# A decoder layer on one core: quantizing the feed-forward weights beside the attention scores, storing through SyncE

## The chip, the cores and the metric

The kernel is one program on one core of a Trainium2 chip. The metric is device time in microseconds (us) of one execution; three executions of the kernel before gave 1202.56, 1204.27 and 1208.85 us, median 1204.27. The engines are named as in the profile: PE is TensorE (PEld its weight loads), DVE is VectorE, ACT is ScalarE, POOL is GpSimd, SP is SyncE. Each engine works through its own instructions in order. Loads and stores between the chip's memory (HBM) and the on-chip memory (SBUF) are issued by SP or by POOL and carried out by the same 16 DMA engines; PE writes only to the eight banks of PSUM.

## The reference

One decoder layer on x of 4 batches x 512 rows x 512 columns, in float32: self-attention, cross-attention, and a feed-forward part whose three weights are first made ternary.

```python
def ternary_quant(w):
    s = jnp.mean(jnp.abs(w))
    q = jnp.clip(jnp.round(w / s), -1.0, 1.0) * s
    return w + jax.lax.stop_gradient(q - w)

# self-attention on layernorm(x), 16 heads; the softmax runs over the 128 columns of q @ k
q = (x @ Wq + bq).reshape(B, T, 128, 16).transpose(0, 3, 2, 1)
k = (x @ Wk + bk).reshape(B, T, 128, 16).transpose(0, 3, 1, 2)
v = (x @ Wv + bv).reshape(B, T, 128, 16).transpose(0, 3, 2, 1)
y = softmax(q @ k / sqrt(128)) @ v            # q @ k is 128 x 128 for each head, y is [B, 16, 128, T]
x = x + y.transpose(0, 2, 1, 3).reshape(B, -1, 2048) @ Wo + bo
# cross-attention of layernorm(x) with the context: 8 heads of 64 rows, softmax over 512 columns
x = x + gamma * vh @ softmax(qh.T @ kh / 8).T
# feed-forward on layernorm(x), hidden size 1365
x = x + (silu(h @ w1q.T) * (h @ w3q.T)) @ w2q.T   # w1q, w3q, w2q = ternary_quant(w1, w3, w2)
```

The ternary weights need two passes over each weight: one that sums absolute values to get the scale, one that compares every element with half the scale.

## The kernel before

**Exact products from halves.** PE multiplies float32r operands. To keep float32 precision each operand is kept as three tiles, called a `Tri`: `h` (a scaled copy, made on ACT), `l` (the rest, on DVE) and `d` (a difference of the two, on DVE; `third_of_weight`, L270, for weights). `products` (L344) runs one 512x512x512 product as two pairs of banks: 16 matmuls of h and l for a pair, a copy of the two banks by ACT (L358), 8 matmuls of d, and `total` (L373) on DVE, which joins copy and bank. It calls a `tick` three times for each pair, six times a product.

**Three phases.** In the *score phase* (L906 to L938) there are 16 steps, `STEPS`, one for each group j of four heads and each batch b. A step computes `keys_of` (one product of the batch's Gram matrix with the key weights of the group), and then the scores of the step before (`scored`, L888), whose softmax weights `turn` (L892) transposes and stores in HBM as `kept_e`. In the *values phase* (L1004 to L1047) there are again 16 steps (b outer, j inner), each with two products (`values_out` with the o weights, `values_of` with the v weights) and `output`, and the cross-attention of the batch before runs beside them in small steps. The *feed-forward phase* (L1107 on) does the rest.

**Work on the side.** A `Side` (L173) is a generator of small steps and a rate: each `tick` of a product takes as many steps as are due. In the score phase the side is `kept_weights` (L286): from the fifth step on (L907), for each of 32 blocks of o and v weights, it loads a raw block (three buffers, two blocks ahead), folds in a mean for v, makes h, l and d (six buffers) and stores all three in HBM (`kept`), all DMAs on POOL (L289, L329), 32 steps over 68 ticks. In the values phase the side `quant` is `quantize` (L661): for w1, w3 and w2 in turn, `quantize_steps` loads 11 or 12 pieces of at most 128x512 through POOL (`staged`, L593, six buffers), sums absolute values on DVE (L628), makes the scales with one small matmul, loads the pieces again, makes them ternary with two DVE instructions (L650, L651) and stores them in HBM (L658). There are 73 steps over 180 ticks. Before each piece, `settle` (L604) multiplies its first column by a one computed from a recent ACT copy (`one_of`, L599), which ties the piece to that copy.

**What sets the order.** SP and POOL issue in program order (L855: `manual_schedule`). PE, ACT and DVE are ordered by a scheduler at build time that follows program order where operands are modelled to be ready; `tc.issue_after(x)` keeps instructions of a block behind instruction x on x's engine. A tile is a buffer of a pool, and whoever writes it anew waits until the last reader is done, a store's landing included. Relevant pools: `made` (six, L324), `raw_k` (`a_kr`, four), the rows `xn` (`a_xn`, eight), the products' weights `a_w` (18, from L976 on) and the staged pieces `a_stage` (six). Weights of the values phase are loaded from `kept` by SP (`weights`, L334), 12 tiles for a product, as far ahead as `a_w` allows.

**Where SP stands.** In the score phase SP loads raw q and k blocks (`raw_all`, L254: a group's whole q after the first scores of that group, its successor's k right behind). At the start of the values phase it loads 12 o tiles, four rows of x, `bo`, 12 v tiles and then `eT` (L1042), for which one of the two `e` buffers must be free: the last two `turn`s come after the first values product (L1017), and their stores go through POOL (L553).

## Time and profile before

| | us |
|---|---|
| median of three runs | 1204.27 |
| lowest, highest | 1202.56, 1208.85 |
| the profiled execution | 1201.91 |
| its span, first to last instruction | 1199.9 |

The granted PE clock is 0.982 of full speed over the span. Busy time of the engines and DMA by phase, read from a table of stretches (74 is the third key product, 293 the end of the score phase, 899 the start of the feed-forward phase):

| stretch, us | PE | DVE | ACT | POOL | clock | DMA share | GB/s |
|---|---|---|---|---|---|---|---|
| 74 to 293 | 215.01 | 155.14 | 93.66 | 84.84 | 0.99 | 0.67 | 223 |
| 293 to 899 | 571.21 | 465.05 | 297.67 | 155.53 | 0.97 | 0.86 | 284 |
| 899 to 1199.9 | 292.40 | 148.78 | 150.25 | 37.18 | 1.00 | 0.19 | 61 |

Over the whole span the page has PE 1148.8 us busy (96%), DVE 817.4, ACT 575.5 and POOL 287.0, and 252.06 MB moved by DMA, 149.21 MB of it in SP's queue and 101.79 MB in POOL's. "Clock" is the share of full PE speed that was granted; "DMA share" is the mean busy share of the 16 DMA engines. PE's busy time includes the modelled tail of pipelined matmuls, so an idle PE is a real gap, but a busy one need not be at full rate; a matmul of 512 columns in these products follows the one before by 0.227 us at full clock and 0.43 at half.

### The profile page before, as it was taken

To read this page: it belongs to the slowest core of one execution; us is meant where nothing else is said; L and a number is where in the kernel's file an instruction comes from. 1 tells how busy PE (TensorE), PEld (TensorE's weight loads), DVE (VectorE), ACT (ScalarE), POOL (GpSimd) and SP (SyncE) were. 2 spreads that over 40 slices of the span, in tenths; PEclk is the share of its full clock that TensorE was granted. 3 is DMA by queue.
4 is the path that set the end of the run, shared out by engine and by line. 5 is a ranking of instruction groups with operands and counts; after the bars stand their busy time and mean duration, and the time that the engine had idled before them with its cause. 6 is when DMAs were issued, how large, how long until landed. Compare 5 with 4: busy or idle time off the path is not lost.

```text
span 1199.9 us, 16588 instructions
## 1 busy us (share of the span) xinstructions
PE 1148.8 (96%) x5406; PEld 888.2 (74%) x5406; DVE 817.4 (68%) x1757; ACT 575.5 (48%) x1156; POOL 287.0 (24%) x515
## 2 busy tenths in 40 slices
PE   8999899999899989999798899998999998999998
PEld 6788788888677667777566676675777776877886
DVE  6657687875577768898759688786886657535242
ACT  4544343443232226557445465563689469733020
POOL 2103363541200233212422221333131311101000
PEclk9999999999899989999899899999999999999999
DMA  9303878787989999977788877898871421221200
GB/s 313 100 9 110 276 262 263 234 278 253 353 315 326 325 297 319 321 224 246 267 270 290 261 239 234 270 342 272 294 232 33 145 80 38 62 79 46 87 1 36
DMA packets 128784, 252.06 MB, mean 210 GB/s; under 512 B 16948, under 2 KB 37732, under 8 KB 128698
## 3 DMA queue, kind: packets, MB, share of 16 engines
q1 hardware_dynamic: 95962, 149.21, 37.5%
q0 software_dynamic: 32736, 101.79, 25.8%
q8 instruction: 43, 0.70, 0.2%
q14 instruction: 43, 0.35, 0.1%
HBM read 196.40 MB, written 54.54 MB: 209 GB/s over the span
## 4 chain that ended last, share of the span: by engine, by line
PE 55%; DMA 15%; issue 12%; DVE 11%; ACT 4%; POOL 4%; SPq 0%; DVEq 0%; POOLq 0%; ACTq 0%
PE h L1124 11%; PE y L1159 7%; PE xo L783 4%; PE xp L127 3%; DMA v_raw<-in_wv_dram 3%; PE po L561 2%; PE sc L520 2%; DMA k_raw<-in_wk_dram 2%; PE xs L739 1%; PE pg L438 1%; PE xs L740 1%; DMA tern_w<-in_w2t_dram 1%; PE pu_3h L351 1%; PE pu_3h L352 1%; DVE xnmax L744 1%
## 5 line engine op out<-in xcount | busy, mean ns | idle before, releaser
L1124 PE MATMUL h<-fxh,t 128*128 128x512 f32 (+1 forms) x352 | 139.9, 398 | 3.2 <-ACT sl L1133 3.2
L1124 PE MATMUL h<-fxl,t 128*128 128x512 f32 (+1 forms) x352 | 137.5, 391 | 0.0
L750 ACT ACTIVATE p<-xs,xnmax 128x512 f32<-128x512 f32 x128 | 87.0, 687 | 68.7 <-PE xp L127 36.4
L744 DVE TENSOR_REDUCE xnmax<-xs 128x1 f32<-128x512 f32 x128 | 84.0, 681 | 10.1 <-PE xs L740 10.1
L1124 PEld LDWEIGHTS h<-fxh,t 128*128 128x128 f32 (+1 forms) x352 | 65.0, 185 | 19.7 <-ACT sl L1133 3.4
L1124 PEld LDWEIGHTS h<-fxl,t 128*128 128x128 f32 (+1 forms) x352 | 65.0, 185 | 14.8 <-DVE fxl L140 0.4
L127 PEld LDWEIGHTS xp<-ident,p 128*128 128x128 f32 x512 | 60.1, 142 | 12.9 <-issue 3.7
L658 POOL DMA_DIRECT2D t_w<-tern_w x43 | 28.6, 666 | 169.9 <-DVE tern_w L651 139.1
L196 ACT ACTIVATE uh<-u 128x512 fp32r<-128x512 f32 x64 | 40.4, 634 | 60.0 <-DVE u L373 59.8
L1159 PE MATMUL y<-t,gh 128*128 128x512 f32 (+1 forms) x176 | 69.0, 392 | 0.0
L1159 PE MATMUL y<-t,gl 128*128 128x512 f32 (+1 forms) x176 | 68.8, 391 | 0.0
L127 PE MATMUL xp<-ident,p 128*128 128x128 f32 x512 | 68.1, 275 | 0.7 <-ACT p L750 0.6
L520 PE MATMUL sc<-y,q_raw 128*128 128x128 f32 x512 | 62.3, 280 | 3.4 <-DVE q_raw L264 3.3
L130 ACT COPY pt<-xp 128x512 f32<-128x512 f32 x96 | 54.7, 590 | 22.5 <-PE xp L127 22.5
L520 PEld LDWEIGHTS sc<-y,q_raw 128*128 128x128 f32 x512 | 61.3, 196 | 5.0 <-DVE q_raw L264 4.0
L1137 DVE SCALAR_TENSOR_TENSOR gf<-h,scales_w,sl 128x512 f32<-128x512 f32 (+1 forms) x44 | 32.9, 747 | 45.2 <-PE h L1124 33.6
L762 ACT ACTIVATE p<-p,xrden 128x512 f32<-128x512 f32 x64 | 47.0, 734 | 27.0 <-DVE xrden L760 26.3
L783 PE MATMUL xo<-pt,vals 128*64 128x512 f32 x256 | 59.5, 599 | 0.2 <-ACT pt L130 0.2
L1133 ACT ACTIVATE sl<-h,scales_w 128x512 f32<-128x512 f32 (+1 forms) x44 | 30.4, 690 | 61.1 <-PE h L1124 61.0
L561 PE MATMUL po<-m,eT 128*128 128x512 f32 x128 | 57.9, 595 | 0.0
L702 POOL DMA_DIRECT2D xd<-x_a x64 | 33.8, 532 | 93.0 <-DVE qs L723 43.1
L739 PE MATMUL xs<-kh,qs 128*128 128x512 f32 x128 | 52.5, 410 | 3.0 <-DVE m L373 1.2
(252 smaller groups left out, 2990.9 us busy)
## 6 DMA issues: line engine op xcount, KB each, us to landing
oh<-kept_oh SPq DMA_DIRECT2D x64, 256.0 KB, 5.1
ol<-kept_ol SPq DMA_DIRECT2D x64, 256.0 KB, 5.2
od<-kept_od SPq DMA_DIRECT2D x64, 256.0 KB, 5.4
vh<-kept_vh SPq DMA_DIRECT2D x64, 256.0 KB, 6.0
vl<-kept_vl SPq DMA_DIRECT2D x64, 256.0 KB, 5.7
vd<-kept_vd SPq DMA_DIRECT2D x64, 256.0 KB, 5.3
xd<-x_a POOLq DMA_DIRECT2D x64, 128.0 KB, 4.3
kd<-in_kv_dram POOLq DMA_DIRECT2D x64, 128.0 KB, 4.2
```

The source lines that it names most:

```text
L127: nc.tensor.transpose(pt[:, ts(k, P)], src[:, ts(k, P)], ident)
L130: nc.scalar.copy(dst, pv)
L196: nc.scalar.mul(tri.h, src, H_OF)
L520: nc.tensor.matmul(sc[:, ts(g, DH)], lhsT=w[k][:, ts(g, DH)], rhs=ys[k][:, ts(g, DH)], start=(k == 0), stop=(k == KC - 1),)
L561: nc.tensor.matmul(po, lhsT=eT[:, ts(g, DH)], rhs=ms[g], start=True, stop=True)
L739: nc.tensor.matmul(sc, lhsT=q[:, ts(m, P)], rhs=kh, start=True, stop=False)
L744: nc.vector.reduce_max(nmax[:, i : i + 1], scs[i], axis=AX.X)
L750: nc.scalar.activation(p, scs[i], AF.Exp, bias=nmax[:, i : i + 1], scale=xscale, accum_out=den[:, i : i + 1],)
L762: nc.scalar.mul(ps[1], ps[1], rden[:, 1:2])
L783: nc.tensor.matmul(po[half, :], lhsT=vals[c][:, l, half], rhs=pt[j][:, l, :], start=(l == 0), stop=(l == NC - 1),)
L1124: nc.tensor.matmul(ph[:r, :], lhsT=t[:, block(i, k)], rhs=fxT[j][:, k, :], start=(k == 0 and j == 0), stop=(k == KC - 1 and j == 1),)
L1159: nc.tensor.matmul(py, lhsT=g[i][j][:r, ts(c, P)], rhs=t2[:r, i, :], start=(i == 0 and j == 0), stop=(i == NHC - 1 and j == 1),)
```

## The change

The quantizing moves from the values phase to the score phase, and the shares of the engines in the side work are set anew:

- `quantize` runs from the third score step on (n == 2), 108 steps over 82 ticks, with three staged pieces instead of six. Its absolute sums are ACT activations (`Abs` with an accumulator) behind the last bank copy, two pieces ahead; the ternary pass stays on DVE, behind the last `total`, one piece ahead, and its stores come one step later. `settle` is no longer called for the pieces. Loads and stores of the pieces stay on POOL.
- `kept_weights` starts at n == 2 instead of 4, with 64 steps over 80 ticks (making and storing a block are steps of their own). `d` is made on POOL; four `made` buffers instead of six; its loads and stores go through SP.
- The stores of `kept_e` go through SP. `turn`s are placed at ticks inside the products; the last two come at ticks 4 and 6 of the first values product.
- A group's last scores follow its last key product at once, the next group's q is loaded there, and q is folded at tick 2. Raw k blocks have three buffers, and the fourth block is loaded later. For the first group it lies in a ninth `xn` buffer.
- The values phase has no quantizing; its weight pool has 24 buffers instead of 18. The rows of x for its first product are loaded and split during the last three score steps.
- Twelve small memsets go from DVE to POOL.

```diff
-    def third_of_weight(tri):
-        nc.vector.tensor_tensor(tri.d, tri.l.bitcast(F32), tri.h.bitcast(F32), ALU.subtract)
+    def third_of_weight(tri, engine=None):
+        (engine or nc.vector).tensor_tensor(
+            tri.d, tri.l.bitcast(F32), tri.h.bitcast(F32), ALU.subtract
+        )
...
     def kept_weights(pool):
-
-        def load(dst, src):
-            nc.gpsimd.dma_start(dst, src)
...
-                *(pool.tile([P, GW], F32R, tag="made", bufs=6, name=f"{n}{p}_{j}_{k}") for p in "hld")
+                *(pool.tile([P, GW], F32R, tag="made", bufs=4, name=f"{n}{p}_{j}_{k}") for p in "hld")
             )
             halves_of_weight(tri.h, tri.l, t, gate)
-            third_of_weight(tri)
+            third_of_weight(tri, nc.gpsimd)
+            yield
             for p, part in zip("hld", (tri.h, tri.l, tri.d)):
-                nc.gpsimd.dma_start(kept[n, j, p][ts(k, P), :], part.bitcast(F32))
+                load(kept[n, j, p][ts(k, P), :], part.bitcast(F32))
             yield
-    KEPT_STEPS = 2 * HG * KC
+    KEPT_STEPS = 2 * 2 * HG * KC
...
-                nc.vector.memset(xs[g][:, D - 1 : D], 1.0)
+                (nc.vector if by_chunk else nc.gpsimd).memset(xs[g][:, D - 1 : D], 1.0)
...
-        nc.gpsimd.dma_start(kept_e[b, j], e)
+        load(kept_e[b, j], e)
...
-    def ahead(pieces, name):
-
-        coming = None
-        for i, (src, t) in enumerate([*pieces, (None, None)]):
-            here, coming = coming, src is not None and (staged(src, f"{name}_{i}"), t, i)
-            if here:
-                settle(here[0])
-                yield here
+    def ahead(pieces, name, by):
+
+        coming = []
+        for i, piece in enumerate([*pieces, *[None] * by]):
+            if piece is not None:
+                coming.append((staged(piece[0], f"{name}_{i}"), piece[1], i))
+            if i >= by:
+                yield coming.pop(0)
...
-        for piece, t, i in ahead(pieces, f"abs_{name}"):
-            nc.vector.tensor_reduce(
-                sums[: piece.shape[0], i : i + 1],
-                piece,
-                AX.X,
-                ALU.add,
-                apply_absolute_value=True,
-            )
+        for piece, t, i in ahead(pieces, f"abs_{name}", 2):
+            r, n = piece.shape
+            spare = stp.tile([P, 512], BF16, tag="above", bufs=1, name=f"spare_{name}_{i}")
+            with tc.issue_after(mark["copied"]):
+                nc.scalar.activation(
+                    spare[:r, :n], piece, AF.Abs, accum_out=sums[:r, i : i + 1]
+                )
             yield
...
-        for piece, t, i in ahead(pieces, f"tern_{name}"):
+        for piece, t, i in ahead(pieces, f"tern_{name}", 1):
             r, n = piece.shape
             above = stp.tile([P, 512], BF16, tag="above", bufs=1, name=f"above_{name}_{i}")
-            nc.vector.tensor_scalar(above[:r, :n], piece, s[:r, 0:1], None, ALU.is_gt)
-            nc.vector.scalar_tensor_tensor(
-                piece, piece, s[:r, 1:2], above[:r, :n], ALU.is_lt, ALU.subtract
-            )
+            with tc.issue_after(mark["total"]):
+                nc.vector.tensor_scalar(above[:r, :n], piece, s[:r, 0:1], None, ALU.is_gt)
+                nc.vector.scalar_tensor_tensor(
+                    piece, piece, s[:r, 1:2], above[:r, :n], ALU.is_lt, ALU.subtract
+                )
+            yield
...
-    QUANTIZE_STEPS = 2 * (6 * KC + NHC) + 3
+    QUANTIZE_STEPS = 3 * (6 * KC + NHC) + 3
...
-    krp = apool("a_kr", 4, phase_a, side="right")
+    krp = apool("a_kr", 3, phase_a, side="right")
...
-    def ticks_with(fold_at):
+    def ticks_of(n):
+        j, b = STEPS[n]
+        due = {4: lambda: turn(n - 2)} if b > 1 else {}
+        if b == 0:
+            due = {4: lambda: turn(n - 2), 6: lambda: turn(n - 1)}
+        if b == 1:
+            due = {2: lambda: queries_folded(j)}
         count = itertools.count(1)
 
         def tick():
             side.tick()
-            if next(count) == fold_at:
-                queries_folded(j)
+            quant.tick()
+            due.get(next(count), lambda: None)()
...
-        if n == 4:
-            xpool.close()
-            ovp = apool("a_ov", 1, phase_a, side="right")
-            side = Side(kept_weights(ovp), KEPT_STEPS, 6 * (len(STEPS) - n) - 4)
+        if n == 2:
+            xpool.close()
+            ovp, stp = (
+                apool(name, bufs, phase_a, side="right", reuse_waits="tile")
+                for name, bufs in (("a_ov", 1), ("a_stage", 3))
+            )
+            side = Side(kept_weights(ovp), KEPT_STEPS, 6 * (len(STEPS) - n) - 4)
+            quant = Side(quantize(), QUANTIZE_STEPS, 6 * (len(STEPS) - n) - 2)
...
-        if n > 0:
+        if b > 0:
             scored(n - 1)
-        if b == 0 and n > 0:
-            raw_q = raw_all("q", j, qp)
-        if b == 0 and j + 1 < HG:
-            raw_k = raw_all("k", j + 1, krp)
+        if b == B - 1:
+            scored(n)
...
-        for n, k in (("a_w", 18), ("a_stage", 6))
+    wp = wpools.enter_context(
+        tc.tile_pool(name="a_w", bufs=24, side="right", reuse_waits="tile")
     )
...
-            u3 = values_out(b, j, x3, wo_tiles, tick)
-            if b == 0 and j == 0:
-                turn(len(STEPS) - 2)
-                turn(len(STEPS) - 1)
-                quant = Side(quantize(), QUANTIZE_STEPS, B * TICKS - 2 * PRODUCT)
+            u3 = values_out(b, j, x3, wo_tiles, tick if b + j > 0 else turning())
```

## The prediction

> **What bounds the kernel now.** I read the page first. TensorE is busy 96% of the span, so only its idle time and the time in which it is granted half its clock can be won. The slices show when:
>
> ```profile
> PEclk9999999999899989999899899999999999999999
> DMA  9303878787989999977788877898871421221200
> ```
>
> The clock dips in the same slices in which the DMA engines are near nine tenths. Next the busy time by 30 us. First two rows of the score phase (74 to 294 us: the third key product starts at 74.1, the first values product at 294.2):
>
> ```profile
> 150.00:180.00 30.00, 30.00 (x170) 26.16 (x169) 25.81 (x54) 14.44 (x37) 18.87 (x34) 1.00 0.78 262
> 240.00:270.00 30.00, 29.43 (x167) 25.33 (x165) 22.38 (x46) 12.71 (x34) 13.05 (x23) 1.00 0.81 278
> ```
>
> Columns: stretch, PE, PEld, VectorE, ScalarE, GpSimd busy, granted clock, DMA share, GB/s. TensorE loses nothing or 0.6 us here. Then the values phase (294 to 899):
>
> ```profile
> 300.00:330.00 30.00, 26.48 (x105) 20.23 (x104) 16.88 (x35) 7.72 (x14) 6.73 (x13) 0.89 0.97 353
> 330.00:360.00 30.00, 30.00 (x127) 23.48 (x125) 21.61 (x44) 9.19 (x16) 1.84 (x4) 1.00 0.90 314
> 420.00:450.00 30.00, 26.65 (x97) 19.75 (x97) 20.59 (x50) 8.08 (x14) 11.98 (x20) 0.90 0.93 298
> 570.00:600.00 30.00, 23.83 (x111) 17.84 (x111) 21.43 (x54) 12.51 (x25) 12.77 (x22) 0.89 0.80 267
> 630.00:660.00 30.00, 26.89 (x115) 20.12 (x116) 27.62 (x59) 17.88 (x38) 8.55 (x15) 0.94 0.88 290
> 660.00:690.00 30.00, 25.77 (x115) 18.85 (x114) 18.53 (x39) 13.46 (x29) 7.96 (x15) 0.89 0.86 261
> 810.00:840.00 30.00, 24.86 (x111) 17.77 (x110) 20.44 (x43) 10.48 (x22) 9.94 (x18) 0.94 0.86 272
> ```
>
> I count a stretch's loss as idle time plus 30 us times the missing clock: for 660 to 690, 4.23 + 3.30 = 7.5 us. The twenty stretches from 300 to 900 sum to 53.4 us. What VectorE waited for there, in total, times and longest:
>
> ```profile
> DVE tern_w L608 <- DMA tern_w<-in_w2t_dram: 12.0, 5, 5.1
> DVE norms L608 <- DMA norms<-norm_a: 9.5, 4, 6.6
> DVE tern_w L608 <- DMA tern_w<-in_w3t_dram: 7.9, 4, 4.3
> DVE tern_w L608 <- DMA tern_w<-in_w1t_dram: 7.9, 4, 4.0
> DVE one L601 <- ACT pu_1t L358: 7.8, 2, 7.1
> ```
>
> With the three rows for `abs_w` (11.2 us) the quantizing's loads hold VectorE up for 39.0 us, and its `one` for 26.6 us over all rows. The chain of waits shows that this reaches TensorE:
>
> ```profile
> 662.55 9.32 DMA abs_w<-in_w2t_dram
> ...
> 672.69 0.75 DVE xc L790
> 673.49 0.79 PE pu_3h L351
> ```
>
> A weight piece lands 9.3 us after its issue; VectorE, which works in order, stands before it; behind it is the `xc` that frees a bank, and then TensorE.
>
> **What leaves the values phase.** All 73 quantizing steps. In VectorE work: 22.2 us of sums (35), 16.7 + 24.7 us of ternary values (35 each), and 70 pairs of `one` and `settle` at 0.146 + 0.160 = 21.4 us; 85 of its 464 busy us there. On GpSimd 70 loads and 43 stores; on the DMA engines 3 x 8.39 MB = 25.2 MB of 172.4 (26 + 8 + 1 pieces of 262, 175 and 174 kB, read twice and written once).
>
> Of the 53.4 us lost I leave some. The 6.8 us of 300 to 330 have another cause: the chain there goes from the last transposed scores through their store (L553) to SyncE, which stood before the `eT` load and then brought `ol` late. Now these stores are SyncE's, ahead of the `v` loads: twelve tiles, 3.1 MB, 8.9 us at the 353 GB/s of that stretch, so this place can cost 0 to 8.9; I keep 6.8, inside that. Of 420 to 450 (6.35) and 570 to 600 (9.47) I keep half, 7.9 us, since the row-norm load (`norms`, longest 6.6) stands beside the weight pieces in both. **Gain 53.4 - 6.8 - 7.9 = 38.7 us.** At least the stretches where the chain runs through `tern_w` or `abs_w` alone: 2.8 (390 to 420) + 4.9 + 7.5 + 6.9 = 22.1. At most all 53.4, with the 24 weight buffers in place of 18 counted in it.
>
> **What the score phase gets.** *Bytes.* It moved 48.83 MB from 74 to 293 us; with the 25.2 it needs 74.0 MB. That is 338 GB/s over its 220 us, and at full share its own rows give 277/0.86 = 322 to 253/0.71 = 356, mean 335 over the six stretches from 120 to 300. So it no longer fits under TensorE with anything to spare. What share can be held? The best here was 0.86, with three pieces ahead; from 300 to 510 it was 0.95, with 18 weight tiles ahead. The new phase has three raw tiles, four made tiles and three staged pieces, so I take the middle, 0.91: 305 GB/s, 74.0/0.305 = 242.6 us, **22.6 us longer**. Bounds: the 353 GB/s seen for 30 us would bring it under TensorE's time, and also take away the phase's own loss (3.42 + 1.80 + 0.57 = 5.8), so -5.8; the 278 GB/s of its own best stretch gives 266 us, +46.
>
> *VectorE.* 155.1 us busy, less the 32 thirds of o and v (11.0 + 11.0) plus 41.4 of ternary work: 174.5 of 219. Durations:
>
> ```profile
> L271 DVE TENSOR_TENSOR od<-ol,oh 128x512 fp32r<-128x512 f32 x16 | 11.0, 690 | 1.1 <-DMA kept_od<-od 0.5 <-DMA kept_vd<-vd 0.2
> L651 DVE SCALAR_TENSOR_TENSOR tern_w<-tern_w,scales_w,above_w 128x512 f32<-128x512 f32 (+2 forms) x35 | 24.7, 707 | 0.5
> L628 DVE TENSOR_REDUCE sums_w<-abs_w 128x1 f32<-128x512 f32 (+2 forms) x35 | 22.2, 642 | 0.6
> ```
>
> The work is hidden by its 45 idle us. Without that cover, each us that it waits for a landing lengthens the phase, since the `total` of the keys (L373) and its bank stand behind. The 39 us of waiting for pieces move here too; this is the same lateness that the bytes price, so it is not added again.
>
> *ScalarE.* The sums become 35 Abs activations with an accumulator. Nearest rows: 634 ns for L196, 687 + 200 ns for L750 with its accumulator read; 22 to 31 us, on 93.7 of 219: hidden.
>
> *GpSimd.* The 150 loads and stores that it issued for o, v and e go to SyncE, the 113 of quantizing come at 0.54 to 0.71 us (69 us), and 32 thirds. No such row exists on GpSimd; its cast of this size takes 614 ns, and two inputs are at most two casts, so 20 to 39 us. At most 108 of 219. But a third beside VectorE can slow VectorE:
>
> ```profile
> L727 DVE SCALAR_TENSOR_TENSOR kl<-kd,norms,kh x32: 730/750/1478, 451.1 to 1039.5; 128x512 fp32r<-128x512 f32 x32
> ```
>
> The 1478 is the one with two tensors in SBUF that overlapped a GpSimd cast; four of L140 that touched one showed nothing. So 0 to 32 x 0.73 = 23 us of VectorE, inside its idle time; I take half and add nothing to the sum. The Trainium skill speaks against this step ("SBUF — State Buffer", "Who interferes with whom"): a VectorE instruction with two SBUF inputs contends with a GpSimd instruction that reads SBUF, and the later one waits for the whole of the other. "GPSIMD Engine Reference", "3. Performance versus the Vector engine", has a two-input add at 1.96 times VectorE's time; as an estimate 0.69 x 1.96 = 1.35 us, 43 us in all, and if VectorE lost all of these the sum would be some 20 us higher than mine.
>
> *SyncE* takes 150 issues at about 0.38 us (`od`, L204), 57 us of 219: hidden. Its order matters more. A made tile's store waits for the third on GpSimd, which can stand behind a ternary store that waits for VectorE and so for a piece's landing; behind it on SyncE wait the raw o and v loads, the next `k` and `q` and the scores' stores. A tick is 14.94/6 = 2.49 us, an item of o or v has 2 x 80/64 = 2.5 ticks = 6.2 us, and raw tiles are asked for two items ahead, 12.4 us against 4.1 to 6.7 us of landing: covered. Four made tiles instead of six mean that `l` of an item reuses `h` of the item before, whose store lands 5 us later: covered by about 1 us; when landings grow, ScalarE and VectorE wait here first (13.0 + 2.8 and 2.4 us now).
>
> *The rest* costs nothing: twelve memsets of 59 ns go to GpSimd; the last batch's scores come right after its keys, with the 3.57 us of the scores before as cover; `q` is folded two ticks earlier but loaded a step earlier.
>
> **Sum**, against the profiled execution's 1201.9 (span 1199.9 and 2.0 around it): 1201.9 + 22.6 - 38.7 = 1185.8. The median, 1204.27, lies 2.4 above that execution, so **1188**.
>
> **Rivals.**
> *The score phase swallows it all.* For it: the DMA engines gave 353 GB/s at 300 to 330, and TensorE lost nothing at 0.95 share from 360 to 390. Against: these were loads asked for far ahead. 1204.3 - 5.8 - 44 (the gain midway to its bound with more DMA freedom) = 1154.
>
> *Slower: three staged pieces cannot turn round fast enough.* Each of the 35 Abs pieces has one step, 82 x 2.49/108 = 1.89 us, and three buffers; a buffer's round is issue 0.54 + landing + 0.89, so at the median landing of 5.6 a piece takes 2.3 us and at the longest, 9.3, 3.6 us. ScalarE stands in order before it, with the copies (L358) that free TensorE's banks behind. At 9.3 us: 35 x (3.6 - 1.89) = 60 us against 38.7, giving 1204.3 + 21 = 1225. It decides from (38.7/35 + 1.89) x 3 - 1.43 = 7.6 us of landing. For it: `k_raw` landed 10.9 us after issue, median, in the score phase with a third less to move. Against: ternary pieces, with three steps each, ask for less and make up.
>
> *Little is relieved.* The values phase's own weight loads and row norms take over the waits: gain 22.1, the phase 22.6 longer: 1205. For it: share 0.86 and 147 MB left. Against: 0.86 falls to 0.73, and 510 to 570 at 0.74 lost nothing.
>
> **How the numbers follow.** Forecast 0.43 (its own range 1168 to 1206), swallowed 0.20, slower 0.25, little relieved 0.12. A measurement here can't tell less than 0.5% (6 us) from no change. Faster, below 1198: 0.36 + 0.20 + 0.03 = 0.59. Same: 0.06 + 0.06 = 0.12. Slower, above 1210: 0.01 + 0.25 + 0.03 = 0.29. The range runs from the swallowing rival's 1153 to 1222, which leaves a tenth on each side.
>
> **What would show it.** Right: the values phase shrinks from 605 to about 566 us, no `tern_w` or `abs_w` wait is left in it, and the clock dips stay only at its start and at the row norms; the score phase ends near 317 us with a DMA share about 0.9, and VectorE or ScalarE wait for pieces in it. Wrong: the score phase ends before 300 us (swallowed) or after 335 us with ScalarE before Abs (slower), or the values phase loses over 30 us still. A VectorE mean of L268 or L651 above 0.9 us would show the thirds on GpSimd as a cost of their own.

## The result, and the profile after

The changed kernel took 1246.4 us, median of four runs (1244.86 to 1247.61), against 1206.56 us for the kernel before, run beside it (four runs, 1202.56 to 1209.46): a ratio of 1.0332, 95% interval 1.0294 to 1.037. It is slower, by 40 us. The forecast was 1188 us, faster, with a range from 1153 to 1222.

The profiled execution shows where. I mark three stretches by the starts of instructions: the score phase from the third key product's first matmul to the first values product, the values phase from there to the first feed-forward matmul, and the rest. (In the kernel before that matmul starts at 877.4 us; the tables ahead of the result end the phase at 899 and so call it 605 us long. Only differences are compared here.)

| | before, us | after, us | forecast of the difference | measured |
|---|---|---|---|---|
| score phase | 220.1 (74.1 to 294.2) | 301.6 (74.4 to 376.0) | +22.6 | +81.5 |
| values phase | 583.2 | 546.6 | -38.7 | -36.6 |
| from the feed-forward on | 322.6 | 322.8 | 0 | +0.2 |
| span | 1199.9 | 1245.4 | -16.1 | +45.5 |

The values phase did what was forecast, within 2 us. The score phase did not. First the slices of the page of the changed kernel, granted clock and share of the DMA engines in tenths:

```profile
PEclk9999978888888999999999999999999999999999
DMA  9257967868768896988655977668691331121200
```

The dips of the clock, spread over the values phase before, now stand together in the slices from about 155 to 405 us. Next its busy time by 30 us (PE, PEld, VectorE, ScalarE, GpSimd, granted clock, DMA share, GB/s); two stretches of the score phase and two of the values phase:

```profile
150.00:180.00 30.00, 20.70 (x93) 16.58 (x92) 20.25 (x40) 8.69 (x20) 12.99 (x17) 0.77 0.75 229
240.00:270.00 30.00, 24.31 (x122) 20.21 (x120) 18.78 (x39) 7.31 (x18) 13.84 (x18) 0.94 0.74 229
650.00:680.00 30.00, 27.54 (x135) 19.93 (x134) 19.14 (x36) 15.44 (x31) 7.89 (x14) 1.00 0.64 215
740.00:770.00 30.00, 30.00 (x140) 21.60 (x139) 25.42 (x48) 18.16 (x39) 3.19 (x6) 1.00 0.61 211
```

In the first row TensorE, which lost nothing in this stretch before, stands idle for 9.3 us and is granted 0.77 of its clock. No engine is busy in its place, and the DMA share is lower than before the change, not higher: 0.75 against 0.78. The same columns for the whole score phase, before and after:

```profile
74.08:294.16 220.08, 216.09 (x1217) 188.26 (x1216) 156.10 (x343) 93.58 (x248) 84.84 (x150) 0.99 0.67 223
74.39:376.00 301.61, 239.05 (x1224) 201.62 (x1222) 181.10 (x392) 116.59 (x318) 108.30 (x145) 0.88 0.77 243
```

Of the 81.5 us TensorE stands idle for 58.6 more, and for 23.0 more it is busy, at a granted clock of 0.88 in place of 0.99. The DMA share is 0.77, with 243 GB/s, where the forecast had taken 0.91 and 305. A phase that is too long, with more bytes to move and no resource full, is one in which engines wait for each other. The waits in it, total in us, times, longest:

```profile
POOL od L277 <- DVE ol L274: 58.3, 8, 34.5
POOL vd L277 <- DVE vl L274: 44.4, 10, 12.8
...
DVE above_w L658 <- DMA tern_w<-in_w3t_dram: 19.3, 8, 4.1
ACT spare_w L639 <- DMA abs_w<-in_w2t_dram: 15.4, 9, 4.6
DVE above_w L658 <- DMA tern_w<-in_w1t_dram: 14.4, 7, 4.5
```

With their other rows, VectorE waited 40.8 us for ternary pieces and ScalarE 35.4 us for pieces of the sums. And GpSimd, which issues those pieces, stood 103 us before the thirds of o and v, waiting for VectorE. One of these waits, 34.5 us, lies almost wholly ahead of the phase: GpSimd stands from 44.0 to 78.5 us before the first third, with the first loads of w1 behind it (start, us, what; idle before in brackets):

```profile
78.50 1.29 POOL L277 TENSOR_TENSOR od<-ol,oh 128x512 fp32r<-128x512 f32 x1 [34.49 <-DVE ol L274]
79.73 1.63 POOL L604 DMA_DIRECT2D abs_w<-in_w1t_dram  x3
```

The other 68 us are spread over the phase. A piece of the chain that ended last (start, us, what) shows how this closes on itself:

```profile
150.46 0.53 POOL od L277
...
151.81 4.10 DMA tern_w<-in_w1t_dram
...
156.01 0.12 DVE above_w L658
...
166.12 0.48 DVE kl L274
...
167.65 0.50 SPq L204
...
168.19 7.39 DMA kept_oh<-oh
...
175.80 0.70 DVE ol L274
...
176.58 1.29 POOL od L277
177.87 0.68 POOL t_w L667
178.54 5.29 DMA t_w<-tern_w
...
184.42 2.58 DMA abs_w<-in_w3t_dram
...
187.08 0.58 ACT spare_w L639 x2
187.66 1.05 ACT e L543 x6
...
189.29 1.12 PE pe L127 x4
```

Read it from the top. Behind a third `od`, GpSimd issues the load of a ternary piece; VectorE stands 2.99 us before that piece's `above_w`, and behind it stands the low half `kl` of a key weight. SyncE waits 6.8 us for this `kl`, because the next raw k block goes into the buffer that `kl` reads, and so issues the store of a high half `oh` late. VectorE cannot write the next low half `ol` into that buffer until the store has landed, 7.39 us later (6.49 us idle). GpSimd stands before the next third `od`, which reads `ol` (10.48 us idle before it); only behind the third does it issue the store of a ternary piece that VectorE had finished before 170; that store frees a staged buffer, into which the next `abs_w` piece is loaded; ScalarE, in order, stands before that piece's Abs with the exponentials `e` behind; and TensorE waits, by way of VectorE, for these with its transposes `pe`. In this piece SyncE was held by VectorE; elsewhere in the phase it is held by GpSimd's thirds, 44.6 us in all, and by ScalarE's copies of the turned scores (its queue's waits):

```profile
SPq L204 <- ACT e L130: 34.0, 7, 10.1
SPq L204 <- POOL od L277: 25.3, 11, 6.3
...
SPq L204 <- POOL vd L277: 19.3, 12, 7.0
...
SPq L204 <- DVE kl L274: 14.1, 2, 7.2
```

So four in-order queues stand in a ring: GpSimd (thirds and the pieces' loads and stores), VectorE, ScalarE and SyncE. That is the theory after the result. Its rivals: bytes (the forecast's own term, only larger), GpSimd's own time, the time that VectorE loses beside a computing GpSimd, the one late start of the loads (79.7 us), and the new places of scores and turns.

### The profile page after: what moved, and what is told of

The parts are those of the page before. It is cut to its first block, busy times and chain, and to the rows that moved or that the text cites. A ratio compares the mean times of both kernels' runs of the same rounds, so it can differ in the third digit from the quotient of the medians.

```text
span 1245.4 us, 16472 instructions
## 1 busy us (share of the span) xinstructions
PE 1155.1 (93%) x5406; PEld 893.6 (72%) x5406; DVE 772.5 (62%) x1538; ACT 596.3 (48%) x1226; POOL 244.3 (20%) x407
## 3 DMA queue, kind: packets, MB, share of 16 engines
q1 hardware_dynamic: 124986, 188.03, 44.6%
## 4 chain that ended last, share of the span: by engine, by line
PE 58%; DMA 14%; DVE 6%; issue 5%; ACT 3%; POOL 3%; SPq 1%; DVEq 0%; POOLq 0%; ACTq 0%
PE h L1167 11%; PE y L1202 6%; PE xo L792 4%; PE xp L127 3%; PE po L569 3%; DMA kept_oh<-oh 2%; PE xs L749 2%; PE xs L748 2%; DMA kd<-in_kv_dram 2%; DMA abs_w<-in_w2t_dram 2%; DMA norm_a<-mv_c 2%; PE sc L528 1%; DMA kept_vh<-vh 1%; PE pm_2d L369 1%; SPq L204 1%
## 5 line engine op out<-in xcount | busy, mean ns | idle before, releaser
L753 DVE TENSOR_REDUCE xnmax<-xs 128x1 f32<-128x512 f32 x128 | 83.8, 681 | 13.5 <-PE xs L749 13.5
L528 PE MATMUL sc<-y,q_raw 128*128 128x128 f32 x512 | 65.2, 290 | 6.9 <-DMA k_raw<-in_wk_dram 5.0
L528 PEld LDWEIGHTS sc<-y,q_raw 128*128 128x128 f32 x512 | 64.3, 206 | 8.4 <-DVE q_raw L270 6.0
L749 PE MATMUL xs<-kl,qs 128*128 128x512 f32 x128 | 50.0, 391 | 0.0
```

The costliest lines, as they stand in the source:

```text
L528: nc.tensor.matmul(sc[:, ts(g, DH)], lhsT=w[k][:, ts(g, DH)], rhs=ys[k][:, ts(g, DH)], start=(k == 0), stop=(k == KC - 1),)
L749: nc.tensor.matmul(sc, lhsT=q[:, ts(m, P)], rhs=kl, start=False, stop=True)
L753: nc.vector.reduce_max(nmax[:, i : i + 1], scs[i], axis=AX.X)
```

## The experiments

One table first. Each kernel's ratio is against runs of the kernel before on the same chip; the phases are those of its one profiled execution, marked as above.

| kernel | time, us | ratio, 95% interval | score phase | values phase |
|---|---|---|---|---|
| before | | | 220.1 | 583.2 |
| after | 1246.4 | 1.0332 (1.0294 to 1.037) | 301.6 | 546.6 |
| quant_back | 1211.33 | 1.0072 (1.0043 to 1.01) | 226.3 | 584.5 |
| dma_only | 1209.76 | 1.0044 (1.0005 to 1.0082) | 262.1 | 545.8 |
| ov_back | 1214.48 | 1.0106 (1.0072 to 1.0139) | 267.5 | 543.2 |
| turns_back | 1241.51 | 1.0313 (1.0269 to 1.0357) | 291.2 | 548.6 |
| pieces_held | 1188.52 | 0.9881 (0.9804 to 0.9959) | 243.5 | 547.7 |
| thirds_dve | 1217.13 | 1.0119 (1.0036 to 1.0202) | 269.8 | 548.0 |
| queue_back | 1234.76 | 1.0266 (1.0181 to 1.035) | 282.2 | 551.0 |
| ov_turns_back | 1219.28 | 1.0137 (1.0024 to 1.025) | 269.4 | 551.8 |
| third_late | 1225.67 | 1.0172 (1.0119 to 1.0225) | 277.1 | 546.1 |
| dma_thirds | 1196.22 | 0.9913 (0.9868 to 0.9958) | 248.4 | 546.4 |
| before_ahead3 | 1183.92 | 0.9824 (0.9777 to 0.9872) | 220.2 | 559.5 |
| split | 1202.44 | 0.9978 (0.996 to 0.9996) | 234.7 | 560.8 |

### Which part of the change costs: one part undone at a time

**quant_back.** The quantizing goes back beside the values, as it was; everything else stays changed.

```diff
-            quant = Side(quantize(), QUANTIZE_STEPS, 6 * (len(STEPS) - n) - 2)
...
+            if b == 0 and j == 0:
+                quant = Side(quantize(), QUANTIZE_STEPS, B * TICKS - 2 * PRODUCT)
```

> The changed kernel with the quantizing put back beside the values as before (six staged pieces, 18 weight buffers, settle); the new making of o and v, its stores through SyncE, the thirds on GpSimd, the new places of turns and scores stay. In the changed kernel the score phase ends at 376 us, before at 294. Late pieces (the quantizing's loads and stores stand in order before the keys' work): ends near 300, total about 1205 to 1215. Making of o and v (four buffers, SyncE's order, thirds): still ends above 350, total 1270 or more, since the values phase loses its 37 us again. DMA rate (the prediction's term): near 300 as well. Turns and scores: above 340.

The score phase is 226.3 us, 6.2 longer than before, and the values phase is back at 584.5. Thirds on GpSimd, four made buffers, stores on SyncE and the moved scores cost 6 us among themselves when nothing of the quantizing stands in the same queues. Late pieces and DMA rate had both expected this; the run doesn't tell them apart.

**dma_only.** Every load and store of the quantizing stays, its arithmetic on the pieces goes.

```diff
-            with tc.issue_after(mark["copied"]):
-                nc.scalar.activation(
-                    spare[:r, :n], piece, AF.Abs, accum_out=sums[:r, i : i + 1]
-                )
...
-            with tc.issue_after(mark["total"]):
-                nc.vector.tensor_scalar(above[:r, :n], piece, s[:r, 0:1], None, ALU.is_gt)
-                nc.vector.scalar_tensor_tensor(
-                    piece, piece, s[:r, 1:2], above[:r, :n], ALU.is_lt, ALU.subtract
-                )
```

> The changed kernel without the arithmetic on the pieces: no absolute sums on ScalarE and no ternary work on VectorE, so the scales are zero and the stored weights are the raw ones; every load and store of the quantizing stays. Late pieces: nothing of VectorE and ScalarE stands before a piece any more, the score phase ends at 300 to 325 us, total about 1175 to 1195. DMA rate: the bytes are all there, it still ends at 365 to 376, total 1235 or more. Making of o and v: 355 to 370.

262.1 us: 39.5 of the 81.5 go. The same bytes at a share of 0.86 and 279 GB/s take much less time when VectorE and ScalarE never stand before a piece and don't work on it. But the phase ends at 337 us, where late pieces alone had been expected to end at 300 to 325: with the arithmetic gone, 35.8 us over quant_back are left, more than the forecast's price for the bytes.

**ov_back** puts the thirds of o and v on VectorE again and their loads and stores on GpSimd; **turns_back** puts scores, turned scores and the folding of q where they were.

```diff
     def kept_weights(pool):
+        def load(dst, src):
+            nc.gpsimd.dma_start(dst, src)
...
-            third_of_weight(tri, nc.gpsimd)
+            third_of_weight(tri)
```

> The changed kernel with the making of o and v as before in its engines: thirds on VectorE, loads and stores through GpSimd (its start at the third step, its pace and four buffers stay). Making of o and v: the score phase ends near 310 us, total about 1180. Late pieces: ends at 360 to 385, total 1230 to 1255. DMA rate: 370 to 380, no difference. Turns and scores: no difference.

The edit of turns_back, at its core:

```diff
-        due = {4: lambda: turn(n - 2)} if b > 1 else {}
...
+        due = {4: lambda: queries_folded(j)} if b == 1 else {}
...
-        if b > 0:
-            scored(n - 1)
-        if b == B - 1:
-            scored(n)
+        if n > 0:
+            scored(n - 1)
...
+        if n > 1:
+            turn(n - 2)
```

> The changed kernel with scores, turns, the load and the folding of q and the last two turns placed as before. Turns and scores (TensorE waits 32.5 us for e before transposes that now stand inside the products): the score phase ends near 340 us, total about 1212. Late pieces, making of o and v or DMA rate: the wait goes elsewhere, it ends at 365 to 380, total within 10 us of 1246.

34.1 and 10.4 us go. ov_back ends at 343 us, between what its making of o and v (310) and late pieces (360 to 385) had been expected to give; no single cause fits. Undone singly, the parts give 75.3 + 39.5 + 34.1 + 10.4 = 159 us of the 81.5: they don't add up, as links of one ring wouldn't. **ov_turns_back** has both edits:

> The changed kernel with the thirds of o and v on VectorE and their loads and stores on GpSimd, and the scores, turns and queries placed as before the change; the quantizing stays beside the scores. Alone these took 34 and 10 us out of the score phase. If both are the same hold-up on SyncE (the turned scores wait behind the stores of o and v): phase 262 to 270, time 1207 to 1216, no better than the first alone. If they are two causes: phase 255 to 260, time 1200 to 1206. If it were DMA rate: 22.6 us over before's phase of 220, 243, remains in every case; a phase well above that, with the DMA share under 0.85, is lateness of the pieces in the in-order queues.

269.4 us, no better than the 267.5 of ov_back alone. Where ov_back has removed the hold-up, the new places of scores and turns cost nothing more.

### Which link of the ring

**thirds_dve** has the second of ov_back's two edits alone, **queue_back** the first.

```diff
-            third_of_weight(tri, nc.gpsimd)
+            third_of_weight(tri)
```

> The changed kernel with the third part of every o and v weight made on VectorE again and not on GpSimd; loads and stores of o and v stay on SyncE. Taking thirds and queue back together took 34 us out of the score phase. If the thirds on GpSimd (32 of 1.32 to 1.35 us, behind VectorE and ahead of the quantizing's own issues on the same engine) are the reason: phase 268 to 275, time 1211 to 1220. If it is the queue on SyncE: phase 295 to 305, time 1238 to 1250. DMA rate: no change, 1240 to 1248.

> The changed kernel with the loads and stores of o and v issued by GpSimd again; the thirds stay on GpSimd. If SyncE's order (a store that waits for its part holds the loads and stores of the turns behind it, and the reverse) is the reason for the 34 us that go with both: phase 268 to 278, time 1211 to 1222. If the thirds on GpSimd are: phase 290 to 305, time 1235 to 1250, worse if the quantizing's issues now also wait behind the stores of o and v. DMA rate: no change, 1240 to 1248.

The thirds alone give 31.8 of the 34.1 us. But the queue alone gives 19.4, and 282.2 lies between the two ranges that I had given (268 to 278, 290 to 305): neither the thirds nor SyncE's order is the reason by itself. On SyncE the stores of made parts stand behind its waits for thirds and for `kl`; taking that link out opens the ring too. With the thirds on VectorE the queue is worth only 2.3 us (269.8 against 267.5). The waits of thirds_dve in the score phase:

```profile
POOL abs_w L604 <- ACT spare_w L639: 53.5, 21, 14.7
...
DVE above_w L658 <- DMA tern_w<-in_w1t_dram: 9.0, 3, 4.3
DVE above_w L658 <- DMA tern_w<-in_w3t_dram: 8.8, 5, 3.9
```

GpSimd now waits mostly for VectorE and ScalarE to be done with the pieces, 53.5 us of it before it can load the next `abs_w`; what these waits cost no run shows. VectorE's wait for ternary pieces is 22.0 us with the row for w2, not 40.8.

**third_late** tells GpSimd's queue from GpSimd's time. The third stays there, one step later, when its input has in most cases been made.

```diff
-            third_of_weight(tri, nc.gpsimd)
             yield
+            third_of_weight(tri, nc.gpsimd)
             for p, part in zip("hld", (tri.h, tri.l, tri.d)):
```

> The changed kernel with the third part of each o and v weight still on GpSimd, but asked for one step later, right ahead of its stores, so that the low half it reads has long been made when GpSimd comes to it. All of the 32 us that the thirds on VectorE took out of the score phase (302 to 270) went with them on GpSimd: if GpSimd's queue stands waiting for VectorE's low half (ol and vl released it for 103 us in all) while the quantizing's loads stand behind it, the phase falls to 270 to 282, time 1213 to 1226. If it is GpSimd's own time (32 of 1.32 to 1.35 us, 43 us) or VectorE slowed beside it (760 and 550 ns against 705 and 469 for each piece), nothing comes back: phase 295 to 305, time 1238 to 1250.

277.1 us: 24.5 of the 31.8 come back although GpSimd does exactly the same work. Its thirds, by shape (busy time, mean ns, idle before):

```profile
L277 POOL TENSOR_TENSOR vd<-vl,vh 128x512 fp32r<-128x512 f32 x16 | 23.3, 1456 | 20.0 <-DVE vl L274 18.9 <-DMA kept_vd<-vd 0.8
...
L277 POOL TENSOR_TENSOR od<-ol,oh 128x512 fp32r<-128x512 f32 x16 | 21.0, 1311 | 25.3 <-DVE ol L274 13.5 <-PE py_0h L358 11.7
```

The wait for VectorE is 18.9 + 13.5 us, where it was 44.4 + 58.3, or 44.4 + 23.8 without the one long wait ahead of the phase. GpSimd's own time (108.3 us busy in the phase in both kernels) and what VectorE loses beside the thirds (some 16 us here, 9 in the changed kernel; below) are no smaller in this run, so neither explains the 24.5. What the 7.3 us that don't come back go with is not shown.

Both runs also let the first loads of w1 go out early, at 45.1 us here and at 44.6 in thirds_dve. That one start is the small part of what they win. Counted from the third key product, the keys of the second group begin 3.5 us earlier in thirds_dve than in the changed kernel, those of the third 11.7, of the fourth 19.2, and the values 31.8; in third_late 7.0, 8.7, 14.6 and 24.5.

**pieces_held.** All of the arithmetic and all stores stay, with the thirds on GpSimd; the 16.8 MB of loads go. Three pieces are loaded once and used in turn.

```diff
-        piece = stp.tile([P, 512], F32, tag="stage", name=name)[:r, :n]
-        nc.gpsimd.dma_start(piece, src)
-        return piece
+        if not held:
+            for i in range(3):
+                held.append(stp.tile([P, 512], F32, tag="stage", name=f"held_{i}"))
+                nc.gpsimd.dma_start(held[-1], w1t[ts(i, P), :512])
+        held.append(held.pop(0))
+        return held[-1][:r, :n]
```

> The changed kernel, but the pieces of the feed-forward weights are not loaded: three 512-wide pieces are loaded once and every Abs, above and ternary step works on one of the three in turn, and every store of a result stays (the feed-forward weights that come out are not the reference's). 16.8 MB of loads leave the score phase, its arithmetic stays. The score phase (from the third key product to the first values product) was 220 us before, 302 after the change, and 262 where the arithmetic alone was left out. Late pieces in an in-order queue: the arithmetic costs nothing once its pieces stand there, phase 225 to 245, time about 1165 to 1190. The arithmetic itself fills VectorE and ScalarE (some 77 us of busy time): phase 260 to 285, time 1200 to 1225. DMA rate alone: 16.8 MB at 243 to 305 GB/s is 55 to 69 us, phase 233 to 247, with the DMA share still near 0.8. Making of o and v (four made buffers, stores on SyncE, thirds on GpSimd): unchanged by this, phase above 265, with waits of VectorE for kept_oh, kept_od and kept_vd still some 15 us.

243.5 us, 17.2 above quant_back, with 8.4 MB of stores in it. So VectorE's and ScalarE's own time is at most 17.2 of the 75.3 us by which the changed kernel lies above quant_back. GpSimd waits as long as ever for VectorE's low halves (73.8 + 53.3 us), and it hurts little, since no load stands behind. This one run can't part bytes from lateness, for both leave with the loads; the next does.

**dma_thirds.** As dma_only, and the thirds on VectorE.

> The changed kernel with the thirds of o and v on VectorE and without the quantizing's arithmetic on its pieces (no Abs, above or ternary step, so the feed-forward weights that come out are not the reference's); every load and store of the quantizing stays. Beside it stand 262 us of score phase with the arithmetic left out and the thirds on GpSimd, 270 with the arithmetic and the thirds on VectorE, 302 with both as changed, 226 with the quantizing taken away. If bytes alone cost what the forecast took (22.6 us) and the rest is the hold-up between GpSimd, VectorE and the pieces: phase 240 to 250, time 1185 to 1197. If bytes cost more than that, because the queues of the phase don't reach 305 GB/s: phase 255 to 264, time 1200 to 1212, with the DMA share 0.86 or more.

248.4 us. Of the ring nothing is left, and the phase is 22.1 us over quant_back: the size that the forecast gave the bytes. Two cautions. quant_back has the thirds on GpSimd, and no run has it with the thirds on VectorE; with them on GpSimd in both kernels the same step is the 35.8 us of dma_only. And with nothing to wait for, GpSimd runs ahead. The loads of its first and last pass (shortest/median/longest ns, first and last start in us):

```profile
L604 POOL DMA_DIRECT2D abs_w<-in_w1t_dram x12: 537/537/542, 44.9 to 57.3; - x12
...
L604 POOL DMA_DIRECT2D tern_w<-in_w2t_dram x11: 534/537/548, 191.6 to 229.3; - x11
```

They begin 30 us before the score phase, and the phase itself moved 68.1 MB against the 74.0 of the forecast. So 22.1 us is nearer to the least that the bytes cost than to the most. dma_only, whose first load is issued at 80.5 us, keeps up with it as far as the keys of the fourth group (187.3 against 188.3 us after the third key product) and loses 14.7 us after that, with loads until 319.7 where dma_thirds has the last at 229.3.

### Was lateness the cause beside the values too?

**before_ahead3** is the kernel before with one edit: pieces are asked for three ahead, not one. The six staged buffers were there.

```diff
-        coming = None
-        for i, (src, t) in enumerate([*pieces, (None, None)]):
-            here, coming = coming, src is not None and (staged(src, f"{name}_{i}"), t, i)
-            if here:
+        coming = []
+        for i, piece in enumerate([*pieces, *[None] * 3]):
+            if piece is not None:
+                coming.append((staged(piece[0], f"{name}_{i}"), piece[1], i))
+            if i >= 3:
+                here = coming.pop(0)
                 settle(here[0])
                 yield here
```

> The kernel before, with the pieces in the values phase asked for three ahead and not one (six staged buffers are there already). If the quantizing's cost beside the values (583 us against 547 without it) is pieces that land late in VectorE's queue, most of the 36 us goes without any move: values phase 550 to 565, time 1168 to 1190. If the values phase is bound by the bytes (DMA share 0.87) or by the engines' time, nothing or little goes: phase 575 to 585, time 1195 to 1208.

1183.92 us (four runs, 1178.77 to 1188.49), 0.9824 of the kernel before: the fastest of all that compute everything. The values phase is 559.5 us; 23.7 us are gone without moving anything, against the 36.6 that the change won there. Two of the stretches that had lost 7.5 and 6.9 us to late pieces, now:

```profile
660.00:690.00 30.00, 30.00 (x141) 21.93 (x139) 27.62 (x59) 17.84 (x37) 6.16 (x12) 0.99 0.78 266
810.00:840.00 30.00, 30.00 (x145) 23.81 (x143) 26.76 (x63) 19.68 (x39) 7.16 (x13) 1.00 0.90 294
```

TensorE has no idle time and keeps its clock, at no fewer bytes. (The work has shifted by up to 24 us against the kernel before, so these two rows illustrate; the length of the phase is the measure.) All that VectorE still waits for ternary pieces in this phase:

```profile
DVE tern_w L608 <- DMA tern_w<-in_w2t_dram: 4.2, 1, 4.2
...
DVE tern_w L608 <- DMA tern_w<-in_w1t_dram: 0.8, 1, 0.8
```

These 5.0 us were 27.8 before. With the pieces of the sums it is 10.1 in place of 39.0.

**split** does only the sums beside the scores, with the thirds on VectorE, and the ternary half beside the values, asked for three ahead.

```diff
-            quant = Side(quantize(), QUANTIZE_STEPS, 6 * (len(STEPS) - n) - 2)
+            quant = Side(quantize(sums_steps), QUANTIZE_STEPS + 3, 6 * (len(STEPS) - n) - 2)
...
+            if b == 0 and j == 0:
+                quant = Side(quantize(ternary_steps), QUANTIZE_STEPS, B * TICKS - 2 * PRODUCT)
```

> The changed kernel with the thirds of o and v on VectorE, only the sums of absolute values (8.4 of 25.2 MB, arithmetic on ScalarE) beside the scores, and the ternary half back beside the values, with its pieces asked for three ahead. If each phase's loss is pieces late in an in-order queue, the ternary half with its wait on VectorE is what costs beside the scores, and the sums are nearly free there: score phase 228 to 245, values phase 550 to 570, time 1178 to 1200. By bytes alone, without lateness: score phase 220 + 8.4 MB at 267 to 305 GB/s less what is idle, 226 to 250, values phase 570 to 580, time 1195 to 1215.

1202.44 us. The values phase is 560.8, no better than the 559.5 with everything in it, and the score phase pays 14.6 us more than before, of which quant_back, without any sums, pays 6.2. The sums are not "nearly free" there, and the time is just outside the 1178 to 1200 that lateness alone had promised. Once the pieces come in time, nothing is won by moving their sums away.

## Why the prediction was wrong

**The relief of the values phase: right.** 36.6 us against 38.7. The reason holds for most of it: lateness of pieces in VectorE's order, since earlier asking alone gives 23.7. What makes up the other 12.9 (fewer bytes, less work on VectorE, 24 weight buffers) was not parted.

**The term that failed is the score phase's, 22.6 us, measured 81.5.** One path through the runs splits it, each figure the difference of two score phases (in the second step the thirds also go to VectorE, in the last they come back):

| step of the path | us | what the prediction made of it |
|---|---|---|
| before to quant_back: o and v, four buffers, SyncE, scores and turns | 226.3 - 220.1 = 6.2 | 0 ("covered", "costs nothing") |
| to dma_thirds: the quantizing's bytes | 248.4 - 226.3 = 22.1 | 22.6 |
| to thirds_dve: its arithmetic, in order on VectorE and ScalarE | 269.8 - 248.4 = 21.4 | 0 ("the same lateness that the bytes price, so it is not added again") |
| to after: thirds on GpSimd among the pieces' loads | 301.6 - 269.8 = 31.8 | 0 ("at most 108 of 219") |

The sizes hold for this order of the steps only. With the arithmetic left out, the thirds on GpSimd cost 13.7 us (262.1 - 248.4), with it 31.8. So 18.1 us appear only where both are there, as they would in a ring that needs both.

*Bytes.* The amount came out near, and part of that is luck: the rate was not as assumed (0.91 and 305 GB/s; 0.82 and 273 in dma_thirds, where the phase moves 68 MB), and with the thirds on GpSimd the same step is 35.8 us.

*Waiting for pieces, not added again.* This is the first failed step: a term put at nothing, which measured 21.4 us. Bytes price how long the DMA engines need; an engine that stands before one piece holds up everything behind it even while the DMA engines have time to spare, as their share of 0.77 shows. How much of the 21.4 us is this waiting and how much the arithmetic's own time is not parted; VectorE still waits 22.0 us for ternary pieces in thirds_dve. The prediction had measured 39 us of this wait in the values phase, and counted on its end there; its move to a phase with three staged buffers instead of six had to appear as a cost.

*GpSimd hidden.* This is the second failed step and the larger, 31.8 us. The thirds take 42.7 us in all:

```profile
L277 POOL TENSOR_TENSOR vd<-vl,vh 128x512 fp32r<-128x512 f32 x16 | 21.6, 1350 | 47.9 <-DVE vl L274 44.4 <-DVE nmax L539 2.9 <-DVE e L554 0.5
...
L277 POOL TENSOR_TENSOR od<-ol,oh 128x512 fp32r<-128x512 f32 x16 | 21.1, 1318 | 58.6 <-DVE ol L274 58.3
```

The first number of each row is what the prediction weighed, against 219 us: no matter, and its 108 us of GpSimd came out (108.3). The second, the idle time before, was not asked about (34.5 of the 58.6 are the wait ahead of the phase). The bound "two casts", 1.23 us, was also too low; the estimate of 1.35 us worked out from the Trainium skill ("GPSIMD Engine Reference", "3. Performance versus the Vector engine") was right, with 1.32 and 1.35 measured. But third_late shows that the time is the small part: 24.5 of 31.8 us come from where the instruction stands.

*SyncE covered.* The prediction wrote down half of the ring: a store waits for the third, the third can stand behind a ternary store, that one waits for a piece. It took a landing of 4.1 to 6.7 us against the lead of 12.4 and called it covered. It did not look the other way, at what stands behind a third on GpSimd: the loads for which VectorE then waits. A lead covers a delay from outside; it doesn't cover a delay that grows out of the lead's own use.

*Four made buffers "covered by about 1 us".* Of VectorE's waits for stores only 7.4 us stand before `ol` for `kept_oh`, but the longest, 6.5 us, is the one in the chain above. What four buffers cost apart from the ring was not tried.

**The rivals.** "Three staged pieces cannot turn round" had the right sign and the right place (ScalarE before Abs, 35.4 us in all), but not the cause. It decides from a landing of 7.6 us, and the median landings of its full pieces were 4.8 to 5.6; they came late because they were issued late. Its 1225 is near the 1217 of thirds_dve, where the thirds are out of the ring and GpSimd waits for staged buffers to come free; more staged pieces were not tried beside the scores, so what three of them cost stays open. "Swallowed" is ruled out (301.6 us), and "little relieved" too (36.6).

**The signs it named.** Right: the values phase falls by about 39 us (36.6), with no wait for pieces left in it. Wrong: a score phase that ends near 317 us at a share of 0.9 (376.0, 0.77). An end "after 335 us with ScalarE before Abs" was named as the sign against it, and came. A mean over 0.9 us for VectorE's low halves (`L268` before) or ternary steps didn't come (682 to 689 and 760 ns): the thirds' cost was not in VectorE's durations, where that sign looked for it.

What stays open: the runs show that breaking the ring at any of several links gives back 19 to 40 us, and not how the 21.4 us of the arithmetic in thirds_dve split between VectorE and ScalarE. Deeper staging beside the scores was not tried.

## What to carry to other kernels

When work is moved, ask of every instruction not only how long it takes and whether its engine has room, but what it waits for and what is queued behind it; then follow that until it ends at TensorE or comes back to itself. Compute that waits for a neighbour doesn't belong on the queue that issues loads for this neighbour, unless its input has long been there: one step later was worth 24.5 us here. And where a profile shows waits for pieces that land late, try asking for them earlier in place before moving the work; two more pieces ahead in buffers that were already there beat the whole rearrangement by 5% (0.9824 against 1.0332, each to the kernel before).

## What the runs showed of the hardware

A third on GpSimd slows some VectorE instructions beside it to about twice their time, and leaves others alone. From the timeline of the changed kernel (start, us):

```profile
162.28 1.93 DVE L658 TENSOR_SCALAR above_w<-tern_w,scales_w 128x512 bf16<-128x512 f32 x1
...
162.64 1.28 POOL L277 TENSOR_TENSOR od<-ol,oh 128x512 fp32r<-128x512 f32 x1
```

`above_w` takes 0.48 us otherwise and here ends after the third, though it began before it. In the same run two of the four ternary steps that overlap a third took 1.62 and 1.66 us against 0.75, one fold of q 1.79 and one of v 1.78 against 0.75. But none of the fourteen key totals `y` (L379, which read the products' bank) that overlap one took more than 0.69 us. Nine instructions lost some 9 us in all: above_w 1.1 + 1.45, tern_w 0.87 + 0.91, and e, gl, kd, q_raw and v_raw 0.7 to 1.1 each. In third_late, where more thirds run beside VectorE, seventeen lost some 16 us, and the ternary mean rose to 887 ns. For instructions with two tensors in SBUF, six of the nine, this agrees with the rule of the Trainium skill that spoke against this step ("SBUF — State Buffer", "Who interferes with whom": they contend with a GpSimd instruction that reads SBUF). `above_w` and `e` read one tensor, which that rule on two inputs doesn't cover; that every third would cost VectorE its whole time, which made some 20 us of it in the prediction, it did not.

Loads and stores of 256 KB in the score phase landed between 2.1 us (`kept_vd`) and 7.7 us (`v_last`) after issue, by the medians of the groups, at a DMA share of 0.77; single stores of `kept_oh` and `kept_vh`, groups with medians of 4.6 and 4.7, stand in the chain with 7.4 and 8.1 us. A lead has to be counted from the slow ones.
